# Where the convolution step of a nine-step software pipeline leaves its gap

## The chip, the core and the metric

The kernel runs on one core of a Trainium2 chip. The metric is device time in microseconds (us) of one execution. Engines are named as in the profile: PE (TensorE matmul), PEld (its weight loads), DVE (VectorE), ACT (ScalarE), POOL (GpSimd) and SP (the engine that here only issues DMAs).

## What is computed

The input is x of shape 16 x 16 x 256 x 256 (batch, channel, row, column), float32. Layer 0, a spectral layer, turns it into a new x and is not touched here. Layer 1, reduced to what matters (`gn` normalizes groups of two channels; all convolutions are padded to the same size; `c` runs over 16 channels; `mish(v) = v*tanh(softplus(v))`):

```python
v   = gn(x)                                        # 16 batches, 16 channels
f   = mish(conv3x3(each channel of v alone, W1))   # 4 features a channel
top, bot = f[rows 0..127], f[rows 128..255]
ker = Wspan * relu(1x1(bot, Wred)) + bspan         # 9 weights for each pixel
ti  = sum over the 9 taps of patches(top) * ker    # the "involution"
shuffled = concat_rows(ti, roll(bot, -1, channel)) # 64 planes of 256 x 256
out = mish(conv3x3(shuffled, W2))                  # the second convolution
gate = sigmoid(conv over channels(mean(out), Weca))# one number a channel
x   = x + v * gate
```

So a batch's gate needs all of the batch's second convolution, and rows of the second convolution need the rows of `ti` and `bot` under them.

## The kernel before, in words

Layer 1 is the function `layer1`. Each batch is cut into nine **units**: unit s covers 30 image rows of the upper half, and the 30 rows 128 further down, of 8 channels; j is the block of rows, h the half of the channels, in the order (0,0), (0,1), (1,0) to (3,1), and then (4,0), the **tail unit** with the last 8 rows for all 16 channels. The tail unit holds half the work of another.

A unit passes through these parts, each a method of `Unit`:

- on creation, `load_rows` issues the loads of its input `z` on SP (ten DMAs, 24 for the tail unit);
- `lower`: first convolution of the lower rows (tile `c`, L1037), then Mish on ACT into `bot` (L1056);
- `reduce`: the 1x1 reduction (`pr`, L1064), Relu on ACT into `r`, and `store_bot`, the DMAs on POOL that put `bot` into the DRAM buffer `cf`;
- `upper(0)`, `upper(1)`: first convolution of the upper rows (L1037), with eight Mish activations each into `wide` (L1085);
- `spread`: eight copies on POOL (L1097, L1098) of shifted columns in `wide`;
- `involution(0)` to `(3)`, one for each feature: for each group of four channels a matmul into `pd` (L1105), a DVE multiply into `t` (L1113) and two DVE adds into `top` (L1116); a full unit has eight such groups and the tail unit four. After the last feature `store_top` issues the DMAs into `cf` on POOL (four for a full unit, L1127; 16 for the tail unit, L1134; one more where j is 0).

The **second convolution** of a batch comes in eight pieces of 32 image rows. `conv2_rows(b, s)` loads a piece's rows from `cf` into one of two buffers `rows2` (one DMA of 2176 KB on SP, L1165). `conv2(b, s, acc)` is a generator in three sections: eight matmuls (L1185) and an ACT copy into `mid`, and half of the sum `pair` on DVE (L1175); then 16 matmuls, DVE `even` and `both`, the other half of `pair`; then 16 matmuls on `pair`, and DVE `odd` (L1212). `pooled` puts Mish over `even` and `odd` and adds their sums to `acc` (L1196).

The **gate** of a batch sums `acc` (L1221), spreads the sum (L1223), multiplies by the channel weights (`pg`, L1237), and takes a sigmoid by a chain of small DVE operations (L1239 to L1245). Then POOL scales the stored x in four pairs of parts `o` (L1253) and writes the output (L1262).

The order on every engine but SP is the program's order, written out by hand in one loop; nothing is rescheduled. Step i of the loop has b, s = divmod(i, 9). In it `now` is unit i, which is in its involution, and `nxt` is unit i+1, which is in its first convolution; the loads of unit i+2 are issued at its start. In between stand the sections of one piece of the second convolution: piece s of batch b-1 in steps s = 0 to 7. In step 8 there is no piece, and the gate of batch b-1 begins. The parts of the step stand in the order lower, involution(0), first section, reduce, upper(0), involution(1), second section, upper(1), spread, involution(2), third section, involution(3). The last batch has its pieces in steps of their own, after all units are done.

PSUM tiles: `c` has two buffers, `pd`, `pr` and `pg` share three (tag "d", pool `psd`), and `c2ps` has one. `top`, `bot` and `z` are double buffered by unit (`z` with two tiles a unit).

Of the kernel before, what the change touches and what calls it, by code (L numbers as in the profile page):

```python
# [10 lines left out]
F32 = mybir.dt.float32  # L11
# [10 lines left out]
P = 128  # L22
# [910 lines left out]
def layer1(ctx, tc, d, zn, cf, mr, nb):  # L933
# [14 lines left out]
    sm = ctx.enter_context(tc.tile_pool(name="l1s", bufs=2))  # L948
# [213 lines left out]
    def conv2_rows(b, s):  # L1162
        t = rows2[(8 * b + s) % 2]
        flat = cf[b % 4].rearrange("(t y) f c x -> (y f c) t x", y=2)
        nc.sync.dma_start(out=t[:, :, 1 : N + 1], in_=flat[:, 16 * s : 16 * s + 17])  # L1165

    def conv2(b, s, acc):

        t = rows2[(8 * b + s) % 2]

        def sums(lo, hi):
            nc.vector.tensor_tensor(  # L1175
                pair[:, lo:hi], t[:, lo:hi, H + 1 :], t[:, lo:hi, : H + 1], ALU.add
            )

        def products(terms, n=0):
            pool, tag = (psd, "d") if n % 2 and b == nb - 1 else (ps2, "c2")  # L1180
            ps = pool.tile([P, 4, H], F32, tag=tag, name="c2ps")
            for i, (w, src, x) in enumerate(terms):
                for blk in range(2):
                    for j in range(4):
                        nc.tensor.matmul(  # L1185
                            ps[32 * j : 32 * j + 32],
                            lhsT=w[:, blk],
                            rhs=src[:, 4 * j + blk : 4 * j + blk + 4, x : x + H],
                            start=(i, blk) == (0, 0),
                            stop=(i, blk) == (len(terms) - 1, 1),  # L1190
                        )
            return ps

        def pooled(y, q):
            k = 2 * s + q
            nc.scalar.activation(y, y, AF.Mish, bias=b2, accum_out=acc[:, k : k + 1])  # L1196

        a = mid[s % 2]
        nc.scalar.copy(a[:, :, :H], products([(c2[:, :, 1], t, H + 1)]))
        sums(0, 9)  # L1200
        yield
        ps = products([(c2[:, :, 0], t, 0), (c2[:, :, 2], t, 1)], 1)
        even = rp.tile([P, 4, H], F32, tag="even", name="even", bufs=2)
        nc.vector.tensor_tensor(even, ps, a[:, :, :H], ALU.add)  # L1204
        both = rp.tile([P, 4, H], F32, tag="both", name="both", bufs=2)
        nc.vector.tensor_tensor(both, ps, a[:, :, 1:], ALU.add)  # L1206
        sums(9, 17)
        yield
        pooled(even, 0)
        ps = products([(c2[:, :, 0], pair, 0), (c2s, pair, 1)])  # L1210
        odd = rp.tile([P, 4, H], F32, tag="odd", name="odd", bufs=2)
        nc.vector.tensor_tensor(odd, ps, both, ALU.subtract)  # L1212
        yield
        pooled(odd, 1)
        yield
# [59 lines left out]
    def begin_unit(i):  # L1275
        if i < len(order):
            b, s = order[i]
            units[i] = Unit(b, i, *blocks[s])

    E = mybir.EngineType  # L1280
    with tc.manual_schedule(engines={E.PE, E.Activation, E.DVE, E.Pool}):
        begin_unit(0)
        begin_unit(1)
        u = units[0]
        u.lower()
        u.reduce()
        u.upper(0)
        u.upper(1)
        u.spread()
        acc, last, second = None, iter(()), iter(())  # L1290
        for i in range(9 * nb + 12):
            b, s = divmod(i, 9)
            now, nxt = units.pop(i, None), units.get(i + 1)
            begin_unit(i + 2)
            if s == 8 and b < nb:
                conv2_rows(b, 0)
            if s < 7 and b and b <= nb:
                conv2_rows(b - 1, s + 1)
            next(last, None)
            if nxt:  # L1300
                nxt.lower()
            next(second, None)
            second = iter(())
            if s == 8 and b and b <= nb:
                last = gate(b - 1, acc)
                next(last)
            if s < 8 and b and b <= nb:
                if s == 0:
                    acc = sm.tile([P, 16], F32, tag="acc", name="acc")
                second = conv2(b - 1, s, acc)  # L1310
            if now:
                now.involution(0)
            next(second, None)
            if nxt:
                nxt.reduce()
            if s == 8:
                next(last, None)
            if nxt:
                nxt.upper(0)
            if now:  # L1320
                now.involution(1)
            next(second, None)
            if nxt:
                nxt.upper(1)
                nxt.spread()
            if now:
                now.involution(2)
            if s == 8:
                next(last, None)
            next(last, None)  # L1330
            next(second, None)
            if now:
                now.involution(3)
# [159 lines left out]
@with_exitstack  # L1493
def forward(ctx, tc, d):
    nb = d["x"].shape[0]
    dram = ctx.enter_context(tc.tile_pool(name="dram", bufs=1, space=DRAM))
    keep = ctx.enter_context(tc.tile_pool(name="keep", bufs=1))
    al = dram.tile([NF, 2, 64, nb, N], F32, name="al")
    bd = dram.tile([nb, P, P], F32, name="bd")
    hd = dram.tile([2, 2, 64, nb, C, N], F32, name="hd")  # L1500
    tabs = (
        dram.tile([P, 2, C, N], F32, name="td"),
        dram.tile([NF, P, 384], F32, name="avd"),
        dram.tile([P, 2, C, N], F32, name="ed"),
    )
    zn = dram.tile([nb, N + 2, C, N + 2], F32, name="zn")
    cf = dram.tile([4, N + 2, 4, C, N], F32, name="cf")
    mr = keep.tile([P, nb, G, 2], F32, name="mr")
    layer0_forward(tc, d, al, bd, tabs)
    layer0_mix(tc, d, al, hd, tabs)  # L1510
    layer0_back(tc, d, hd, bd, zn, mr, tabs[2])
    layer1(tc, d, zn, cf, mr, nb)
# [25 lines left out]
```

## Time and profile before

| what | us |
|---|---|
| median of 3 runs | 7067.28 (7063.57 to 7080.53) |
| the profiled execution | 7081.88, its span 7080.1 |
| layer 1 begins, about | 3560 |
| a full step, second convolution in it | 24.29 |
| a batch's nine steps | 211.5 to 214.3 |

The span is the time from the first to the last recorded instruction. A profile line of a group gives its source line, engine, operation, tiles (out<-in), shape and count, then the busy time, the mean duration, and the idle time of the engine before it with what ended it. In a timeline each row is a run of equal instructions: its start, the time from its start to its end, engine, line and tiles, and in brackets the idle time before it. One matmul of the program appears as two instructions of the chip; some records are missing.

### The profile page before, as it was taken

What the parts mean: (1) busy time and instruction counts of PE and PEld (TensorE: products, weight loads), DVE (VectorE), ACT (ScalarE), POOL (GpSimd) and SP (SyncE); (2) the same over time, 40 slices, a digit from 0 to 9 for tenths busy, and PEclk for the clock granted to TensorE, in tenths of its full rate; (3) what the DMA queues carried; (4) which work ended last, traced back from release to release, by engine and by line L of the source; (5) the groups of instructions that cost most, each with busy time, mean ns of one, the idle gap of its engine ahead of it and who ended that gap; (6) DMA issues with size and microseconds to landing.
All of it is one profiled execution on the core that took longest, in us unless ns stands there. A gap on an engine that the chain in (4) does not pass through costs nothing. (4 is left out here: it accounts for less than half of the span.)

```text
span 7080.1 us, 144599 instructions
## 1 busy us (share of the span) xinstructions
PE 6544.7 (92%) x55592; PEld 3663.3 (52%) x55592; DVE 5608.9 (79%) x10346; ACT 3835.5 (54%) x5996; POOL 3521.3 (50%) x4614
## 2 busy tenths in 40 slices
PE   7889999899999998899979999999999999999996
PEld 5777778666667666677733333333333333333331
DVE  8999985466667666688878888888888888888885
ACT  2223333365666665322266666666666676666671
POOL 2334445412222222466655666667666667665663
PEclk9899999999999999999989999999999999999998
DMA  3344444433333333699968888889888889888886
GB/s 99 112 115 123 125 120 123 132 95 92 100 99 102 98 96 92 207 326 326 326 191 248 260 257 269 277 278 282 268 257 265 277 281 278 277 258 264 277 272 212
DMA packets 716083, 1443.41 MB, mean 204 GB/s; under 512 B 98954, under 2 KB 525254, under 8 KB 673638
## 3 DMA queue, kind: packets, MB, share of 16 engines
q1 hardware_dynamic: 567206, 959.76, 44.3%
q0 software_dynamic: 148192, 474.40, 21.3%
q8 instruction: 444, 7.27, 0.4%
q14 instruction: 241, 1.97, 0.1%
HBM read 877.12 MB, written 556.47 MB: 202 GB/s over the span
## 5 line engine op out<-in xcount | busy, mean ns | idle before, releaser
L1085 ACT ACTIVATE wide<-c,b 32x512 f32<-32x512 f32 x2176 | 1477.6, 679 | 314.0 <-PE c L1037 265.2
L1116 DVE TENSOR_TENSOR top<-pd,t 32x512 f32<-32x512 f32 x2176 | 1504.0, 691 | 55.8 <-DMA cf<-top 3.2
L1037 PE MATMUL c<-z,w 102*128 102x512 f32 x2048 | 996.4, 618 | 110.5 <-ACT wide L1085 89.0
L1113 DVE TENSOR_TENSOR t<-pd,r 64x512 f32<-64x512 f32 x1088 | 743.8, 684 | 349.0 <-PE pd L1105 322.8
L1097 POOL COPY wide<-wide 32x1031 f32<-32x1031 f32 (+1 forms) x576 | 581.2, 1009 | 882.6 <-ACT wide L1085 855.5
L1105 PE MATMUL pd<-wide,dw 128*128 128x512 f32 x2048 | 994.4, 607 | 13.0 <-DVE top L1116 12.0
L720 POOL DMA_DIRECT2D hd<-h x512 | 323.5, 639 | 1207.1 <-DVE h L713 1182.6
L1037 PEld LDWEIGHTS c<-z,w 102*128 102x128 f32 x2048 | 370.6, 191 | 695.2 <-issue 457.9
L1185 PE MATMUL c2ps<-rows,c 128*32 128x512 f32 x6144 | 721.9, 602 | 5.6 <-DVE odd L1212 5.6
L1105 PEld LDWEIGHTS pd<-wide,dw 128*128 128x128 f32 x2048 | 382.8, 193 | 576.5 <-issue 417.2
L1056 ACT ACTIVATE bot<-c,b 128x512 f32<-128x512 f32 x544 | 343.9, 683 | 462.2 <-issue 383.3
L1098 POOL COPY wide<-wide 32x1031 f32<-32x1031 f32 (+1 forms) x576 | 574.0, 997 | 33.5
L700 PE MATMUL ph<-ix,yt 64*128 64x256 f32 x4128 | 506.6, 393 | 6.1 <-issue 5.4
L643 PE MATMUL ps<-tt,lt 128*64 128x256 f32 x4224 | 495.4, 385 | 13.3 <-DMA tt<-td 10.4
L313 PE MATMUL px<-wxn,u 128*64 128x256 f32 x4224 | 482.9, 380 | 8.1 <-ACT o L320 8.1
L207 PE MATMUL pu<-fy,eo 128*128 128x128 f32 x2048 | 427.0, 292 | 26.4 <-DVE u L224 21.8
L700 PEld LDWEIGHTS ph<-ix,yt 64*128 64x128 f32 x4128 | 395.9, 191 | 93.7 <-issue 46.1
L1185 PEld LDWEIGHTS c2ps<-rows,c 128*32 128x32 f32 x6144 | 175.4, 109 | 513.3 <-issue 407.8
L873 POOL TENSOR_TENSOR x<-x,o 128x512 f32<-128x512 f32 x256 | 323.7, 1265 | 217.4 <-DVE o L872 199.3
L607 DVE TENSOR_SCALAR alb<-alc,m 128x1024 f32<-128x1024 f32 x330 | 420.0, 1397 | 0.0
L214 PE MATMUL pv<-at,eo 128*128 128x128 f32 x2048 | 413.9, 285 | 0.0
L651 DVE COPY s<-ps 128x512 f32<-128x512 f32 x264 | 265.4, 1023 | 186.9 <-PE ps L643 169.7
(220 smaller groups left out, 11732.0 us busy)
## 6 DMA issues: line engine op xcount, KB each, us to landing
rows<-cf SPq DMA_DIRECT2D x128, 2176.0 KB
z<-zn SPq DMA_DIRECT2D x768, 257.8 KB
cf<-top POOLq DMA_DIRECT2D x512, 240.0 KB, 6.8
cf<-bot POOLq DMA_DIRECT2D x96, 840.0 KB, 11.0
alc<-al SPq DMA_DIRECT2D x264, 256.0 KB
zn<-zb SPq DMA_DIRECT2D x128, 516.0 KB
o<-zn SPq DMA_DIRECT2D x128, 516.0 KB
z<-in_x SPq DMA_DIRECT2D x64, 1024.0 KB
```

The source lines that it names most:

```text
L207: nc.tensor.matmul(pu[:, xh, e].rearrange("p v m -> p (v m)"), lhsT=lhs, rhs=fy[:, e], start=True, stop=True,)
L313: nc.tensor.matmul(ps[64 * k : 64 * k + 64, :, h], lhsT=u[:, h, part, g0 + j + k].rearrange("p f c -> p (f c)"), rhs=wxn[:, h, part], star ...
L643: nc.tensor.matmul(ps[64 * h : 64 * h + 64, v], lhsT=lt[:, h, k, 1 - v : 3 - v].rearrange("p l f c -> p (l f c)"), rhs=tt[:, h, k], start= ...
L700: nc.tensor.matmul(ph[q][:, e], lhsT=yt[lanes, i].rearrange("p t k -> p (t k)"), rhs=ix[lanes, i], start=n == 0, stop=n == 3,)
L1037: nc.tensor.matmul(ps[:, a], lhsT=w, rhs=z[:k, c : c + 2, 0:N], start=True, stop=True)
L1085: nc.scalar.activation(self.feat[64 - 32 * q : 96 - 32 * q, f, self.groups[g], :H], ps[q][32 * f : 32 * f + 32], AF.Mish, bias=b1[0][32 * ...
L1097: nc.gpsimd.tensor_copy(flat[0:32, f, 1:m], flat[64:96, f, 0 : m - 1])
L1098: nc.gpsimd.tensor_copy(flat[96:128, f, 0 : m - 1], flat[32:64, f, 1:m])
L1105: nc.tensor.matmul(ps, lhsT=dwt if self.tail else dw, rhs=self.feat[:, f, cs, :H], start=True, stop=True,)
L1113: nc.vector.tensor_tensor(t[64:128], ps[:64], self.r[:, cs], ALU.mult)
L1116: nc.vector.tensor_tensor(self.top[32 * f : 32 * f + 32, cs, q], ps[lanes], t[lanes], ALU.add)
L1185: nc.tensor.matmul(ps[32 * j : 32 * j + 32], lhsT=w[:, blk], rhs=src[:, 4 * j + blk : 4 * j + blk + 4, x : x + H], start=(i, blk) == (0, 0 ...
```

## The change

The pieces of the second convolution move one step towards the units. Piece 0 of batch b stands in step 8 of batch b itself, beside its tail unit, and pieces 1 to 7 in steps 0 to 6 of the next batch. The step without a piece is step 7 in place of step 8, and the gate's sections move with it. The loads of the rows move by one step, too: pieces 0 and 1 are loaded in steps 7 and 8, and pieces 2 to 7 in steps 0 to 5. The loop is one step shorter. No compute instruction or DMA is added or removed; their order changes, and on SP and POOL the DMAs of `rows`, `o` and the output move past those of the units.

```diff
-        for i in range(9 * nb + 12):
+        for i in range(9 * nb + 11):
             b, s = divmod(i, 9)
             now, nxt = units.pop(i, None), units.get(i + 1)
             begin_unit(i + 2)
-            if s == 8 and b < nb:
-                conv2_rows(b, 0)
-            if s < 7 and b and b <= nb:
-                conv2_rows(b - 1, s + 1)
+
+            if s >= 7 and b < nb:
+                conv2_rows(b, s - 7)
+            if s < 6 and b and b <= nb:
+                conv2_rows(b - 1, s + 2)
             next(last, None)
             if nxt:
                 nxt.lower()
             next(second, None)
             second = iter(())
-            if s == 8 and b and b <= nb:
+            if s == 7 and b and b <= nb:
                 last = gate(b - 1, acc)
                 next(last)
-            if s < 8 and b and b <= nb:
-                if s == 0:
-                    acc = sm.tile([P, 16], F32, tag="acc", name="acc")
-                second = conv2(b - 1, s, acc)
+            if s == 8 and b < nb:
+                acc = sm.tile([P, 16], F32, tag="acc", name="acc")
+                second = conv2(b, 0, acc)
+            if s < 7 and b and b <= nb:
+                second = conv2(b - 1, s + 1, acc)
             if now:
                 now.involution(0)
             next(second, None)
             if nxt:
                 nxt.reduce()
-            if s == 8:
+            if s == 7:
                 next(last, None)
             if nxt:
                 nxt.upper(0)
...
             if now:
                 now.involution(2)
-            if s == 8:
+            if s == 7:
                 next(last, None)
```

## The prediction

> **What bounds the kernel now.** I read the page first: which engine carries the chain that ended last, and which engines are full.
>
> ```profile
> PE 6544.7 (92%) x55592; PEld 3663.3 (52%) x55592; DVE 5608.9 (79%) x10346; ACT 3835.5 (54%) x5996; POOL 3521.3 (50%) x4614
> PE c2ps L1185 16%; PE c L1037 13%; PE pd L1105 13%; ACT wide L1085 3%; PE pr L1064 2%; DVE top L1116 0%; DVE pair L1175 0%; DVE t L1113 0%; DMA cf<-top 0%; ACT odd L1196 0%; ACT bot L1056 0%; DVE even L1204 0%; POOL o L1253 0%; DVE both L1206 0%; DMA out_dram<-o 0%
> ```
>
> Layer 1 is a chain of its own matmuls; the one other entry of weight is ACT's `wide` (3%). Next come stretches, one for each of steps 6, 7, 8 and 0 at a batch boundary (columns: stretch, length, busy PE, PEld, DVE, ACT, POOL with counts, granted clock, DMA share, GB/s):
>
> ```profile
> 4974.64:4998.93 24.29, 24.29 (x121) 8.35 (x120) 21.02 (x30) 16.86 (x27) 11.29 (x15) 1.00 0.71 229
> 4998.93:5020.52 21.59, 21.59 (x110) 7.41 (x109) 20.75 (x30) 9.49 (x16) 15.78 (x26) 1.00 0.88 261
> 5020.52:5034.83 14.31, 12.59 (x35) 4.86 (x33) 11.66 (x31) 10.05 (x17) 1.56 (x3) 1.00 0.88 292
> 5034.83:5065.74 30.91, 27.26 (x121) 9.44 (x122) 22.36 (x33) 21.56 (x33) 27.28 (x40) 0.89 0.88 245
> ```
>
> Step 6 is pure PE. The loss sits in step 8, which has no piece of the second convolution, and in the step 0 that inherits it. PE's timeline there:
>
> ```profile
> 5020.52 3.60 PE L1037 MATMUL c<-z,w 102*128 102x512 f32 x8
> 5026.78 0.37 PE L1237 MATMUL pg<-wca,totals 128*128 128x16 f32 x2 [0.27 <-DVE totals L1223]
> 5034.83 1.98 PE L1037 MATMUL c<-z,w 102*128 102x512 f32 x4 [1.46 <-ACT wide L1085]
> 5040.47 3.78 PE L1037 MATMUL c<-z,w 102*128 102x512 f32 x4 [3.65 <-ACT wide L1085]
> 5044.04 2.71 PE L1105 MATMUL pd<-wide,dw 128*128 128x512 f32 x4
> ```
>
> ACT has the 16 `wide` of a full unit (5029.18 to 5040.42 in its own timeline) and PE has too little beside them, so it waits 1.46 and 3.65 us for a `c` buffer. The two rows after the long wait cost 3.78 and 2.71 us where the same rows elsewhere cost about 1.8. Fine stretches say why:
>
> ```profile
> 5040.50:5044.00 3.50, 3.50 (x4) 1.47 (x5) 0.00 (x0) 1.20 (x2) 3.33 (x4) 0.50 1.11 356
> 5044.00:5048.00 4.00, 4.00 (x17) 1.29 (x19) 1.95 (x3) 1.26 (x2) 3.55 (x7) 0.79 1.10 334
> ```
>
> After the wait the clock is half for 3 to 4 us.
>
> [...]
>
> **The work without its waits.** A full step is 24.29. Its parts from PE's timeline: a group of `c` 1.72, a `pd` 0.905, the piece 1.77 + 3.61 + 3.57 = 8.95, `pr` 1.0. Step 7 lacks two groups of `c`: 20.85. Step 8 lacks four `pd` (3.62) and the piece and has `pg` (0.33): 12.05. So the nine steps hold 7 x 24.29 + 20.85 + 12.05 = 202.9. The gate's matmul repeats at 211.5 to 214.3 us, median 211.9: 9.0 are lost in each batch (8.6 in the best).
>
> **After, step 7.** Nothing is removed in sum; PE's work of the nine steps stays 202.9. Step 7 now has 20.85 - 8.95 + 0.33 = 12.2 of PE work, and eight groups and the gate on DVE. Durations from DVE's timeline:
>
> ```profile
> 5000.42 0.68 DVE L1113 TENSOR_TENSOR t<-pd,r 64x512 f32<-64x512 f32 x1
> 5002.57 0.68 DVE L1113 TENSOR_TENSOR t<-pd,r 64x512 f32<-64x512 f32 x1
> 5026.15 0.17 DVE L1221 TENSOR_REDUCE total<-acc 128x1 f32<-128x16 f32 x1 [1.75 <-ACT odd L1196]
> 5026.67 0.68 DVE L1113 TENSOR_TENSOR t<-pd,r 64x512 f32<-64x512 f32 x1
> 5028.81 0.17 DVE L1239 TENSOR_SCALAR gate<-pg 128x16 f32<-128x16 f32 x1
> 5032.15 0.68 DVE L1113 TENSOR_TENSOR t<-pd,r 64x512 f32<-64x512 f32 x1
> ```
>
> A group takes 2.15 (5000.42 to 5002.57), `total` and `totals` 0.52, the chain of the sigmoid 3.34 (5028.81 to 5032.15). Counted from the start of step 7: ACT ends the last `odd` at 3.93 (as at 5002.86 now) and DVE ends step 6's groups at 3.64, so `total` starts at about 3.96, and the first group at 4.48; two groups to 8.78; sigmoid to 12.12; groups 3 to 5 to 18.57. The eighth `pd` needs the buffer of the fifth group: it runs from 18.6 to 19.5. So step 7 takes 19.5, of which 7.3 are lost, in pieces: near 2.0 before `pg` (its buffer is the first group's), 2.8 behind the sigmoid, and twice 1.2. The same pattern without the gate stands in batch 0, whose step 7 has no piece even now:
>
> ```profile
> 3731.54 1.88 PE L1037 MATMUL c<-z,w1t 120*128 120x512 f32 x4
> 3747.77 1.10 PE L1105 MATMUL pd<-wide,dw 128*128 128x512 f32 x2 [1.05 <-DVE top L1116]
> 3748.70 3.60 PE L1037 MATMUL c<-z,w 102*128 102x512 f32 x8
> ```
>
> 17.16 us for eight groups of 2.15: DVE sets it, and the clock is 1.00 there.
>
> **After, steps 8 and 0.** Step 8 gets the piece: 24.29 - 3.62 = 20.67. ACT needs 16 x 0.70 + 4 x 0.6 + 2 x 0.7 + 0.6 + 0.9 = 16.5 in it, under PE's 20.7, so the waits for `wide` go; 8.95 us of piece cover the 5.1. DVE enters step 8 6.9 us late (its last group of step 7 ends at 26.4), but has only four groups and 5 us of piece there; the second half of `pair` ends within 0.1 us of need. If this cover failed it would cost the old 1.46 + 3.65. Step 0 is 24.29. Sum of the three steps: 19.5 + 20.7 + 24.3 = 64.5. Now they take 211.9 less six full steps (145.7) = 66.2, or 65.8 in the best batch. So a batch gains 1.3 to 1.7, if the clock stays whole. It may not: [...] A half window that falls within step 7 is hidden behind DVE; one that reaches 1 to 2 us into step 8 costs half of that, up to 0.9. Bounds for the clock: 0 and 0.9 a batch, with nothing to exclude a second half window (1.7 more). I take 0.5, and a gain of 0.9 a batch: 15 boundaries, **-13.5 us**.
>
> **Moved DMAs.** Loads of rows are the trace's only 1024-byte packets of their queue; they end 7 to 27 us before their first matmul in all batches before the last. Pieces 0 to 2 need stores of units 0 to 7, long issued or 14 us ahead. Piece 3 is the exposed one: its load needs the tail unit's `top`, and is issued at step 1 where it was step 2. POOL in step 8: eight copies of `spread` (8.8) from 16.8 us after the step's start, where `upper(1)` begins to give `wide`, to 25.6; two scaled parts and output DMAs (6.6, from 5044.44 to 5051.09 now), then the 16 stores (9.5, from 5051.09 to 5060.6), to 42 and landing 4 later: 46, where step 1 starts at 45. SP stands some 8 us at that load, with `o` and the next `z` behind it, which are needed 20 us later. A load takes 9 to 20 us from there, in the trace's packets, and PE wants it at 74: slack 8 to 19. Costed at nothing; beyond that slack each us late costs 1 us in each batch. `top`'s buffer is reused at 49.8, 4 us behind these stores.
>
> **The end.** Now from step 8 of the last batch (6929.31) to the second piece (6956.56): 27.25 us. After: the second piece starts when the first one's `odd` is done. DVE reaches 34.6 (from step 7's start) with the halves of `pair`, PE needs 3.6, `odd` 1: 39.3, which is 19.8 after step 7. That saves 7.4; a half clock takes 1, and piece 3's load, which starts right behind the tail's stores even now (first packet 6969.2, last store issued 6965.8; 2.5 us slack), about 3. Bounds 0 and 8; I take **-3.5 us**.
>
> Sum -17. The profiled execution (7081.88) is 14.6 over the median, and some 7 of that lie in four batches with longer periods; the gain is the same on both, so from the median: 7067.3 - 17 = **7050**; from the profiled one 7065.
>
> **Rivals.**
> 1. *The trade is even*: the clock loss returns in step 8 (0.9 and some of a second window) and eats the batch gain; only 0 to 5 us at the end remain: 7064. For it: a 2.8 us gap; against: batch 0 held 1.00 with gaps of 1.05.
> 2. *Better*: the clock never drops and the irregular longer periods (up to 214.3) go with the step-8 knot: 15 x 1.7 + 7 = 32: 7035. Against: one of those is a wait for a store (`top` behind DMA, 3.2 us) in the middle of a batch.
> 3. *Slower, by POOL's late tail stores*: at step 1, piece 3's load, if the stores land 8 to 19 us later than worked out, PE waits. To lose 0.3% this has to cost (21 + 17)/15 = 2.5 us a batch beyond the slack; at 4 us it is 7067 + 60 - 17 = 7110. For it: DMA is full (share 1.02) in the gate's steps, POOL is overfull in step 8 (25.9 us of work in 20.7). Against: POOL is more overfull now (14.3) and catches up in one step.
>
> **Chances.** Forecast 0.48 (own range 7036 to 7062), rival 1 0.24, rival 2 0.12, rival 3 0.16. A change under 0.3% (21 us; bounds 7046 and 7088) can't be told from none. Faster: rival 2 and near half of the forecast: 0.34. Slower: most of rival 3: 0.14. The range 7030 to 7088 leaves out the rest of rival 2 and of rival 3.
>
> **What would show it.** Right: PE's waits for `wide` in step 8 gone; in step 7 waits for `top` and for the gate of 1 to 3 us, step 7 near 19.5 and step 8 near 20.7; period near 210.5 to 211. Half clock inside step 7 or absent. Wrong: a step 7 over 21, PE waiting for `rows` or for `spread` in steps 1 or 2, or a half clock well inside step 8.

## The result and the profile after

| | before | after |
|---|---|---|
| median | 7073.90 us (4 runs, 7063.57 to 7082.51) | 7124.31 us (4 runs, 7113.31 to 7128.94) |
| the profiled execution, its span | 7081.88, 7080.1 | 7128.94, 7127.1 |
| a batch's nine steps, mean of batches 2 to 14 | 212.1 | 215.6 |

The ratio is 1.0068, with a 95% interval of 1.0056 to 1.0080. The change made the kernel slower by 50 us, where 17 us of gain were forecast.

**Engines and chain.** First the page of the kernel after: the line of busy times, and the chain that ended last.

```profile
PE 6556.4 (92%) x55592; PEld 3657.8 (51%) x55592; DVE 5604.6 (79%) x10346; ACT 3835.4 (54%) x5996; POOL 3502.2 (49%) x4614
...
PE c2ps L1185 13%; PE c L1037 11%; PE pd L1105 10%; DVE top L1116 2%; DMA cf<-top 2%; PE pr L1064 1%; DMA out_dram<-o 1%; POOL o L1253 1%; DVE t L1113 1%; POOL wide L1098 1%; POOL wide L1097 1%; ACT wide L1085 0%; POOL cf L1134 0%; DVE exp_n L782 0%; ACT bot L1056 0%
```

The work is the same. What is new is in the chain: ACT's `wide` (3% before) is gone, and in its place stand the stores of `top`, the output DMA, POOL's scaling of `o` and POOL's copies in `wide`. All of these are POOL's, or issued by POOL. DVE's `top` has risen from 0 to 2%.

**Where the time goes.** Stretches of the kernel after, one for each of steps 7, 8, 0 and 1 at one batch boundary (stretch, length, busy PE, PEld, DVE, ACT, POOL with counts, granted clock, DMA share, GB/s):

```profile
5233.17:5252.79 19.62, 14.50 (x31) 4.99 (x30) 18.09 (x41) 8.07 (x13) 13.32 (x23) 0.91 1.02 330
5252.79:5273.64 20.85, 20.85 (x113) 6.84 (x112) 16.49 (x25) 14.98 (x23) 13.36 (x21) 1.00 1.02 327
5273.64:5297.92 24.28, 24.28 (x122) 8.45 (x120) 19.95 (x27) 18.06 (x30) 18.00 (x28) 1.00 0.92 292
5297.92:5330.40 32.48, 27.32 (x122) 8.95 (x121) 21.05 (x30) 16.86 (x27) 24.95 (x34) 0.89 0.88 252
```

The first three rows are what the forecast worked on, and at this boundary they are as forecast: 19.62, 20.85 and 24.28. It is an extreme case: its steps 7 and 8 are among the shortest, and its step 1 loses the most of all batches. The loss is in the last row, step 1, which has no part in the edit's gap: 32.48 us for a step of 24.28, of which 5.16 are idle and 3.0 are matmuls at half clock (27.32 busy where 24.28 is the work). Averaged over batches 2 to 14 (from one unit's first `bot` to the next one's, on ACT), the steps read:

```
step        8      0      1      2      3      4      5      6      7      sum
before    17.95  26.62  24.28  24.47  24.28  24.27  24.28  24.28  21.72   212.14
after     20.84  24.27  26.82  25.98  24.28  24.28  24.27  24.28  20.63   215.64
```

Steps 7, 8 and 0 together gained 0.55 by this count. Steps 1 and 2 lost 4.2 us over a clean 24.28 each. They lose in batches 2 to 15, so 14 x 4.2 = 59 us. In batch 1, which has no gate running into it from the batch before, they lose nothing. Added up over the 14 batches, step 1 loses 39 us and step 2 22 (the kernel before loses 2.7, once). In five of them the wait brings half clock with it; these five lose 6.0 to 8.2 us each, 33 us of the 61.

**What PE waits for in step 1.** PE's timeline of the kernel after, two rows from the start of that step:

```profile
5297.92 3.60 PE L1037 MATMUL c<-z,w 102*128 102x512 f32 x8
...
5306.68 3.78 PE L1105 MATMUL pd<-wide,dw 128*128 128x512 f32 x4 [5.16 <-POOL wide L1098]
```

The first `pd` of the step waits 5.16 us for POOL's copies in `wide` (`spread`), and then its matmuls take 3.78 us where 1.8 is usual. So POOL is late. Its timeline before, from the output DMAs in step 8 to the next unit's `spread` (step 8 began at 5020.52):

```profile
5050.28 0.81 POOL L1262 DMA_DIRECT2D out_dram<-o  x1 [0.30 <-POOL o L1253]
5051.09 3.04 POOL L1134 DMA_DIRECT2D cf<-top  x6
5054.82 0.51 POOL L1134 DMA_DIRECT2D cf<-top  x1 [0.69 <-DMA out_dram<-o]
5056.11 4.47 POOL L1134 DMA_DIRECT2D cf<-top  x9 [0.78 <-DMA out_dram<-o]
5060.57 1.06 POOL L1157 DMA_DIRECT2D cf<-bot  x2
5061.68 1.03 POOL L1097 COPY wide<-wide 32x1031 f32<-32x1031 f32 x1
```

And the same stretch of POOL's timeline after (step 8 began at 5252.79):

```profile
5284.92 0.81 POOL L1262 DMA_DIRECT2D out_dram<-o  x1 [0.30 <-POOL o L1253]
5285.73 3.05 POOL L1134 DMA_DIRECT2D cf<-top  x6
5290.58 0.51 POOL L1134 DMA_DIRECT2D cf<-top  x1 [1.81 <-DMA out_dram<-o]
5294.60 4.03 POOL L1134 DMA_DIRECT2D cf<-top  x8 [3.51 <-DMA out_dram<-o]
5300.05 0.50 POOL L1134 DMA_DIRECT2D cf<-top  x1 [1.43 <-DMA cf<-top]
5300.55 0.54 POOL L1157 DMA_DIRECT2D cf<-bot  x1
5303.92 0.54 POOL L1157 DMA_DIRECT2D cf<-bot  x1 [2.83 <-issue]
5304.50 1.03 POOL L1097 COPY wide<-wide 32x1031 f32<-32x1031 f32 x1
```

The same instructions stand in the same order in both: two outputs, the tail unit's 16 stores, two stores of `bot`, then the copies that PE needs. The difference is in the brackets. Issues on POOL waited for an earlier DMA to land (0.69 and 0.78 us before; 1.81, 3.51 and 1.43 after), and everything behind them on POOL waited too, copies included. The earlier DMA is nearly always the one eight issues before: in layer 1 of these two traces POOL never has more than eight DMAs issued and not yet landed, and 134 of the 138 such waits in the kernel after end within 0.5 us of that landing (74 of 75 before). These eight are the "slots" of the expectations below; whether the chip or the program sets them is not shown. So the ninth DMA from the first output on, here the tail unit's seventh store, stood for 1.81 us, until that output had landed. Counted from the start of step 8:

| POOL | before | after | adds to the delay |
|---|---|---|---|
| the 16 stores begin | 30.6 | 32.9 | +2.3 |
| the 16 stores are issued | 40.1 | 47.8 | +5.4 |
| `spread` begins | 41.2 | 51.7 | +2.8 |

Step 1 starts at 45 in both, and its first `pd` wants the copies at about 48.8. Before, they were there with about 5 us to spare (first two copies done at 43.3); after, they are 5 us late. In the mean of batches 1 to 14 the 16 stores take 9.1 us before and 14.1 after, and `spread` begins at 41.9 and 48.8. The 2.8 us of the last row, a wait for which the profile shows no releaser, belong to this boundary. Output DMAs land in 8.1 us before and 9.5 after, with DMA shares of 0.88 in step 8 before and 1.02 in steps 7 and 8 after.

**What PE waits for in step 2.** Here it is another waiter on the same queue. Late copies and scaled parts also put off the stores of unit 0's `top`, which stand behind them on POOL, and DVE needs that buffer again in step 2 of the loop. Batch 10 of the kernel after, whose step 2 starts at 5757.20 and loses 2.5 us:

```profile
5750.56 2.04 POOL L1127 DMA_DIRECT2D cf<-top  x4
5766.57 1.39 DVE L1116 TENSOR_TENSOR top<-pd,t 32x512 f32<-32x512 f32 x2 [3.71 <-DMA cf<-top]
5768.11 1.10 PE L1105 MATMUL pd<-wide,dw 128*128 128x512 f32 x2 [0.51 <-DVE top L1116]
5770.25 1.10 PE L1105 MATMUL pd<-wide,dw 128*128 128x512 f32 x2 [1.05 <-DVE top L1116]
```

DVE waits 2.2 to 4.5 us in this way in the ten batches whose step 2 loses time, and at most 1.0 in the four that lose nothing there. Before, it happened once (3.2 us).

### The profile page after: what moved, and what is told of

Read it like the earlier page. It is cut to its first block, busy times and chain, and to the rows that moved or that the text cites. A ratio compares the mean times of both kernels' runs of the same rounds, so it can differ in the third digit from the quotient of the medians.

```text
span 7127.1 us, 144607 instructions
## 1 busy us (share of the span) xinstructions
PE 6556.4 (92%) x55592; PEld 3657.8 (51%) x55592; DVE 5604.6 (79%) x10346; ACT 3835.4 (54%) x5996; POOL 3502.2 (49%) x4614
## 4 chain that ended last, share of the span: by engine, by line
PE 35%; DVE 4%; POOL 4%; DMA 4%; issue 2%; ACT 1%; SPq 0%; POOLq 0%; DVEq 0%; ACTq 0%
PE c2ps L1185 13%; PE c L1037 11%; PE pd L1105 10%; DVE top L1116 2%; DMA cf<-top 2%; PE pr L1064 1%; DMA out_dram<-o 1%; POOL o L1253 1%; DVE t L1113 1%; POOL wide L1098 1%; POOL wide L1097 1%; ACT wide L1085 0%; POOL cf L1134 0%; DVE exp_n L782 0%; ACT bot L1056 0%
## 5 line engine op out<-in xcount | busy, mean ns | idle before, releaser
L1116 DVE TENSOR_TENSOR top<-pd,t 32x512 f32<-32x512 f32 x2176 | 1504.2, 691 | 89.9 <-DMA cf<-top 37.7
L1105 PE MATMUL pd<-wide,dw 128*128 128x512 f32 x2048 | 1028.2, 621 | 119.7 <-DVE top L1116 87.6
L1037 PE MATMUL c<-z,w 102*128 102x512 f32 x2048 | 982.6, 612 | 33.3 <-DMA z<-zn 20.8
L207 PE MATMUL pu<-fy,eo 128*128 128x128 f32 x2048 | 430.8, 294 | 26.8 <-DVE u L224 21.5
```

The lines of the kernel that those rows point to most:

```text
L207: nc.tensor.matmul(pu[:, xh, e].rearrange("p v m -> p (v m)"), lhsT=lhs, rhs=fy[:, e], start=True, stop=True,)
L1037: nc.tensor.matmul(ps[:, a], lhsT=w, rhs=z[:k, c : c + 2, 0:N], start=True, stop=True)
L1105: nc.tensor.matmul(ps, lhsT=dwt if self.tail else dw, rhs=self.feat[:, f, cs, :H], start=True, stop=True,)
L1116: nc.vector.tensor_tensor(self.top[32 * f : 32 * f + 32, cs, q], ps[lanes], t[lanes], ALU.add)
```

## The experiments

Three theories stood at the start.

- **A**: the gate's output DMAs stand ahead of the tail's stores on POOL, and the stores wait for them to land; put elsewhere or taken out, the stall goes.
- **B**: the stall comes with the pieces' new place (their row loads now fill DMA around the tail unit); it stays wherever the gate and its outputs stand.
- **C**: it is POOL's own time, the scaling of `o` above all, that makes `spread` late.

The expectations call runs 1, 2, 5 and 6 below e1, e2, f1 and f0. All diffs are against the kernel after, unless said otherwise; where one lengthens the loop, the steps added at its end do nothing but finish the generator of the last gate.

**1. The pieces moved, the gate left in step 8.**

```diff
-        for i in range(9 * nb + 11):
+        for i in range(9 * nb + 12):
...
-            if s == 7 and b and b <= nb:
+            if s == 8 and b and b <= nb:
                 last = gate(b - 1, acc)
...
-            if s == 7:
+            if s == 8:
                 next(last, None)
```

(the last two lines in both places)

> The pieces of the second convolution stand as in the changed kernel, the gate and its parts stay in step 8 as before. Theory A (what the changed kernel lost is POOL's: the tail unit's 16 stores wait for in-flight slots behind the gate's output DMAs, which the change put a step earlier into a full DMA, and the next spread stands behind them): with the outputs back in their old steps the 4.4 us a batch that PE lost in steps 1 and 2 mostly go, and step 7 loses the sigmoid's 3.3 us and the wait for the sum as well (from 19.6 to about 15.3 to 16): 64.75 - 3.6 = 61 for steps 7, 8 and 0, a batch of about 207, and a time of 6985 to 7010, faster than before. Theory B (the row loads, moved beside the tail unit, fill the DMA and hold the stores whatever the gate does): step 7 is short too, but steps 1 and 2 keep 3 to 5 us of waits a batch: 7045 to 7065.

Measured: 7062.88 us, 0.9986 of the kernel before (0.9977 to 0.9994). By the number this is B's. But the sum hides two things: step 7 falls to 16.1 us, and steps 1 to 3 still lose 4.4 us over clean ones. So the stall is there with the outputs back where they were, which A had not foreseen. The order of parts and stores on POOL is that of the kernel before, where `spread` had some 5 us of slack; with the piece in step 8 and its row loads a step earlier this slack is used up: the 16 stores take 13.7 us (batches 1 to 14), nearly the 14.1 of the kernel after. So most of their lengthening comes with the pieces' move, and not with the earlier outputs. PE's waits for POOL's copies, from the list of waits between 3950 and 6900 us (what waits, for what: us in total, times, longest), of this kernel:

```profile
PE pd L1105 <- DVE top L1116: 56.0, 61, 2.3
PE pd L1105 <- POOL wide L1098: 21.1, 19, 4.0
```

and of the kernel after:

```profile
PE pd L1105 <- DVE top L1116: 70.0, 39, 3.6
PE pd L1105 <- POOL wide L1098: 28.2, 19, 5.2
```

19 waits for the copies in both; the kernel before has none of note. DVE's waits for stores to land, to reuse `top`, are 63.7 us here and 37.7 in the kernel after.

**2. The gate in step 7, its scaled parts one step later.** In `gate`, behind `scale`:

```diff
         nc.vector.tensor_tensor(scale, gate, std2[:, b], ALU.add)
         yield
+        yield
+        yield
         for k in range(0, 8, 2):
...
-        for i in range(9 * nb + 11):
+        for i in range(9 * nb + 12):
```

> The changed kernel, with two empty turns after the gate's sigmoid, so that the scaling and the output DMAs come one step later, in the steps they had before; sum, sigmoid and pieces stay in step 7 and 8. Theory A: the stalls of steps 1 and 2 shrink from 4.4 to under 1.5 us a batch: 7124 less 45 to 65, so 7060 to 7080. Theory B: no change, 7115 to 7130. Step 7 stays at 19.6 us in both.

Measured: 7100.19 us, 1.0039 (1.0025 to 1.0053), between the two. Steps 1 to 3 lose 2.4 us instead of 4.2. PE's waits for copies fall from 28.2 to 9.8 us, but DVE's waits to reuse `top` do not (48.5 us). One step is not enough: the first two outputs still stand ahead of the tail's stores, which take 11.8 us, and the next two ahead of the copies issued in step 1.

**3. No output.** This leaves out the output DMAs of batches 0 to 14; the scaling stays.

```diff
-                nc.gpsimd.dma_start(out=dst.rearrange("c y x -> y c x"), in_=o[:, :, 1 : N + 1])
+                if b == nb - 1:
+                    nc.gpsimd.dma_start(
+                        out=dst.rearrange("c y x -> y c x"), in_=o[:, :, 1 : N + 1]
+                    )
```

> The changed kernel without the output DMAs of the first 15 batches (their result is not written; all else, the scaling on POOL too, stays). Theory A: with the outputs out of the in-flight slots the 16 stores take about 9 us, spread is in time, PE's stalls in steps 1 and 2 go: 7124 - 60 = 7060 to 7070. Theory C (POOL has simply too much work of its own in step 8, slots or not): 3 us of the 10 us of delay go with the issues, the stalls stay near 3 us a batch: 7095 to 7115.

Measured: 7067.19 us, 0.9989 (0.9980 to 0.9998). Steps 1 and 2 are clean (24.30 and 24.28). A's number, though not quite A's reason: the 16 stores begin 3.2 us earlier, but take 12.6 us, where 9 were expected. C's number is missed, and all the scaling is still on POOL.

**4. No scaling.** This leaves out POOL's scaling in batches 0 to 14; the outputs stay, unscaled.

```diff
-                for i in range(4):
-                    eng = nc.vector if i and b == nb - 1 else nc.gpsimd
+                for i in range(4 if b == nb - 1 else 0):
+                    eng = nc.vector if i else nc.gpsimd
```

> The changed kernel without POOL's scaling of x in the first 15 batches (the parts are written out as they were loaded; all DMAs stay). POOL has 4.4 us less before the tail unit's stores. Theory C: the delay of spread falls by those 4.4 us and the stalls nearly go: 7065 to 7080. Theory A: the output DMAs are issued earlier but land late all the same, and half of the 4.4 us comes back as waits for slots: 7080 to 7105.

Measured: 7068.97 us, 0.9991 (0.9983 to 1.0000), and steps 1 and 2 lose only 0.25 us. That is C's number, not A's. Read with the run before it: either of the two, taken away, is enough. Here the waits of POOL's issues for outputs to land rose (the tail's stores 69.0 us in all, where after has 52.8; the 16 take 17.2 us), and yet `spread` was on time, because the scaling ahead of it was gone and the stores began 6.3 us earlier. So neither theory alone is right. What counts is the sum in POOL's queue ahead of `spread`: scaling, issues and waits for landings together.

**5. The gate in step 7, its parts from step 0 on.** Four yields in place of the two of run 2, and a loop of `9 * nb + 13`. No part or output stands ahead of the tail's stores any more; the row loads stay where the kernel after has them.

> The changed kernel with four empty turns after the sigmoid: scaling and output DMAs come in steps 0 to 3 of the next batch, two steps later than in the changed kernel, so that in step 8 POOL has only the spread and the tail unit's stores. Theory A/C (POOL's queue in step 8): the tail's stores begin 6.6 us earlier and find the slots free, the next spread is in time, PE's waits in steps 1 and 2 (4.2 us a batch) go to under 0.7: 7124 - 55 = 7060 to 7075, as without outputs. Theory B (the DMA engines are full in these steps whatever POOL does, and e2 only spread it): waits of 2 us or more stay, and come in steps 2 to 4: 7090 to 7105. Step 7 stays near 20.6.

Measured: 7063.52 us, 0.9985 (0.9978 to 0.9991) of a kernel before of 7075.10. Steps 1 and 2 are 24.27 each. POOL's timeline of this kernel, tail's stores to `spread`:

```profile
5250.87 3.99 POOL L1134 DMA_DIRECT2D cf<-top  x8
5259.01 2.00 POOL L1134 DMA_DIRECT2D cf<-top  x4 [4.15 <-DMA cf<-top]
5261.28 2.00 POOL L1134 DMA_DIRECT2D cf<-top  x4 [0.27 <-issue]
5263.28 1.07 POOL L1157 DMA_DIRECT2D cf<-bot  x2
5264.62 1.03 POOL L1097 COPY wide<-wide 32x1031 f32<-32x1031 f32 x1 [0.27 <-ACT wide L1085]
```

The stores still wait 4.2 us for a landing, now that of the first of them, eight issues earlier, but they start behind `spread`'s last copy, with no part in between, and the next copies wait for ACT and not for POOL. B as it stands falls: the row loads are all here, and the stores take 12.4 us (9.1 before), but begin 7.7 us earlier than in the kernel after, so PE loses nothing in steps 1 and 2, and DVE no longer waits to reuse `top`. Against this kernel, the one after is slower by 60.8 us by the medians (and 63.4 by the spans), which is the 59 us of steps 1 and 2.

**6. The same with the gate in step 8**, that is runs 1 and 5 together: step 8 for the gate, two extra yields, and a loop of `9 * nb + 13`.

> The kernel of e1 (pieces moved, gate in step 8) with two empty turns after the sigmoid: scaling and output in steps 0 to 3. Theory A/C: e1's short step 7 (16.1) stays, and its 4.4 us of waits in steps 1 to 3 go to about 1: a batch near 208.5, 7063 - 45 = 7010 to 7025, faster than both kernels. Theory B: a batch that is shorter by PE's sum meets a full DMA, waits of 3 to 4 us stay: 7050 to 7065.

Measured: **7002.31 us** (4 runs, 6999.22 to 7013.02), **0.9895** (0.9875 to 0.9916). It beats both kernels. Against run 5 step 7 falls from 20.8 to 16.3 and step 8 rises from 20.8 to 21.5: 3.8 us a batch, which is close to the DVE time of the gate worked out in the prediction (3.34 for the sigmoid's chain and 0.52 for the sums), moved from a step that DVE bounds into one with over 4 us of DVE to spare (step 8 of the kernel after: 16.49 us busy in 20.85). PE's timeline of this kernel in step 7 and at the gate in step 8:

```profile
5194.15 1.10 PE L1105 MATMUL pd<-wide,dw 128*128 128x512 f32 x2 [0.88 <-DVE top L1116]
...
5198.44 2.04 PE L1105 MATMUL pd<-wide,dw 128*128 128x512 f32 x2 [1.05 <-DVE top L1116]
5200.28 4.33 PE L1037 MATMUL c<-z,w 102*128 102x512 f32 x8
5208.14 0.40 PE L1237 MATMUL pg<-wca,totals 128*128 128x16 f32 x2
```

The waits are in pieces of 1 us, and `pg` waits for nothing.

**7. The control: the kernel before, with the parts later.** Two extra yields and a loop of `9 * nb + 13` in the kernel before.

> The kernel before with the two empty turns of f0: sum, sigmoid and pieces as before, scaling and output one step later, in steps 0 to 3. If f0's gain comes from the moved pieces with POOL kept clear, this alone does little, since before has no wait for spread at the boundary: 7060 to 7078. If the later outputs are a gain by themselves: 7000 to 7040.

Measured: 7069.35 us, 0.9997 (0.9991 to 1.0004). Later parts alone gain nothing; they only matter once step 8 holds a piece.

**8. Is the wait behind the sigmoid dear beyond its length?** Run 5, with three matmuls that nobody reads in step 7, behind `involution(1)`. They go to the buffer of `c2ps`, which is free in that step.

```diff
             if now:
                 now.involution(1)
+            if s == 7 and 0 < b < nb:
+                spare = ps2.tile([P, 4, H], F32, tag="c2", name="spare")
+                for _ in range(3):
+                    nc.tensor.matmul(
+                        spare, lhsT=dw, rhs=now.feat[:, 0, 0:4, :H], start=True, stop=True
+                    )
```

> The kernel of f1 (changed, parts from step 0) with three idle matmuls of 128 x 512 in step 7 after involution(1), into the free buffer of c2ps; nothing reads them. They fill 2.6 of the 3.6 us for which PE waits behind the sigmoid. If the half clock that follows this wait is what makes step 7 last 20.8 where the durations on DVE add up to 19.6: the half clock goes, step 7 falls to about 19.7, and the time from 7063.5 to about 7047 in spite of more work on PE. If the step is longer for another reason: 7063 to 7070.

Measured: 7045.24 us (4 runs, 7042.32 to 7056.64), 0.9962 (0.9947 to 0.9977), 18 us under run 5 by the medians, 16 by the ratios to the kernel before; the two profiled executions differ by 9, this one's being the slowest of its four. PE's timeline of run 5 behind the sigmoid:

```profile
5220.53 1.81 PE L1105 MATMUL pd<-wide,dw 128*128 128x512 f32 x2 [3.59 <-DVE top L1116]
5222.67 1.85 PE L1105 MATMUL pd<-wide,dw 128*128 128x512 f32 x2 [0.33 <-DVE top L1116]
```

and of this one:

```profile
5216.45 2.74 PE L1331 MATMUL spare<-wide,dw 128*128 128x512 f32 x6
5219.02 1.02 PE L1105 MATMUL pd<-wide,dw 128*128 128x512 f32 x2
5221.06 1.10 PE L1105 MATMUL pd<-wide,dw 128*128 128x512 f32 x2 [1.01 <-DVE top L1116]
```

The spare matmuls fill the gap, the same `pd` takes 1.02 in place of 1.81, and the half-clock time between 3800 and 6900 us (from the trace's clock records) falls from 81.9 to 20.5 us. Step 7, from its first `c` to the next, is 19.6 in 9 of the batches 1 to 14 and 20.4 or 20.5 in the other 5; in run 5 it is 19.6 in only 4.

## Why the prediction was wrong

**Step 7: right but for the clock, wrong in its pieces.** Forecast 19.5, measured 19.6 where the clock is whole at its end. But PE's waits are not 2.0, 2.8 and twice 1.2. PE's timeline of the kernel after, from `pr` to the next step:

```profile
5236.92 1.05 PE L1064 MATMUL pr<-bot,wr 128*32 128x512 f32 x4 [0.15 <-DVE top L1116]
5238.76 0.40 PE L1237 MATMUL pg<-wca,totals 128*128 128x16 f32 x2 [0.78 <-ACT r L1073]
...
5247.57 3.89 PE L1105 MATMUL pd<-wide,dw 128*128 128x512 f32 x4 [3.62 <-DVE top L1116]
5251.86 1.10 PE L1105 MATMUL pd<-wide,dw 128*128 128x512 f32 x2 [0.41 <-DVE top L1116]
5252.79 3.60 PE L1037 MATMUL c<-z,w 102*128 102x512 f32 x8
```

The wait ahead of `pg` is 0.78, and the one behind the sigmoid 3.62, with half clock behind it: four matmul instructions in 3.89 us, where 1.88 is usual. A fine stretch of the same trace:

```profile
5247.50:5251.00 3.50, 3.30 (x4) 0.97 (x4) 3.39 (x5) 0.00 (x0) 3.21 (x6) 0.52 0.85 233
```

DVE hides this inside step 7 unless the half clock reaches the step's end; then step 7 takes 20.5 (8 of the 14 batches 1 to 14), and step 8, too, begins at half clock. The mean of step 7 is 20.2.

**Steps 8 and 0: right with a whole clock.** 20.85 and 24.28, for 20.7 and 24.3. The waits for ACT's `wide` (71.5 us in all before) are gone. But the mean of step 8 is 21.3 (20.8 to 22.0 from its first `c` to the next step's), since the half clock runs into it. So the clock costs 0.6 in step 7 and 0.4 in step 8: 1.0 a batch, where 0.5, its author's estimate, was taken. This term was mis-sized, and a batch gains 0.5 in these steps, for 0.9. A hint stood in the prediction's own stretches: the half clock that it read as 3 to 4 us lasts from 5038.88 to 5045.70, 6.8 us, in the trace's clock records, 5.2 of them after the wait.

**The end: right.** From step 7 of the last batch to the second piece of the last convolution it was 48.8 us and is 43.1: 5.7 saved, where 3.5 for the end and 2.1 for step 7 itself make 5.6. From there on both kernels take 123.5 us.

**"Moved DMAs ... Costed at nothing": this step failed.** It saw POOL's queue in step 8, with the copies ending at 25.6 (measured 25.1) and the parts at 32.2 (measured 32.9). Then it went wrong twice. It priced the 16 stores at 9.5 us, as they had stood before, and so had them issued at 42; with their waits for landings they were issued at 47.8 (on average they took 14.1 us). And it asked who waits for these stores (the row load of piece 3, the reuse of their own `top`), but not who stands behind them on POOL: the next unit's `spread`, whose slack was only 5 us, and behind that the stores of unit 0's `top`, which DVE awaits in step 2. In place of nothing this cost 59 us. PE waiting for `spread` in steps 1 or 2 does stand among the prediction's signs of being wrong, and it came true, but the working gave that wait no time and no slack. The waits for landings stood on POOL itself, 3.51 us of them for one output, ahead of the copies behind it.

The row load of piece 3 was no cause: in all batches before the last the rows are 3.5 to 25 us ahead of their first matmul. `top` was the smaller of the two causes, with step 2's 22 us against step 1's 39; DVE's waits to reuse it came to 37.7 us, where before had 3.2.

**Rival 3** had the place (the tail's stores on POOL) and the wrong waiter. That its size fits (4 us a batch, 7110) is luck: it was an example, not worked out. What was held against it, that POOL is overfull before too and catches up in one step, was the weak argument: before, it caught up because the tail's stores waited only 1.5 us.

**The account.** The profiled executions differ by 47.0 us. By PE's first `c` of each step, +59.1 of it lie in steps 1 and 2 of batches 2 to 15, -7.0 in steps 7, 8 and 0 at the 14 boundaries behind batches 1 to 14 (-0.5 each), +2.1 at the boundary behind batch 0, where no gate runs and the piece is only added, -5.8 from step 7 of the last batch on, and -1.4 ahead of all this.

**What stays open.** Run 1 shows that the 16 stores take nearly as long (13.7 us for 14.1) with the outputs in their old steps. What it is in the pieces' move that lengthens them, the row loads beside the tail unit or the changed lengths of the steps, was not separated. Run 5 shows only that without the parts ahead it costs nothing.

## What to carry to other kernels

When DMAs are issued from an engine that also computes, price its whole queue: here an issue's wait for a landing was a wait of every copy and store behind it, and at the boundary shown the waits of the tail's stores came to 1.5 us before and 6.8 after, with a DMA share of 0.51 while they were issued before (5051.09 to 5060.57) and 0.77 after (5285.73 to 5300.55). When a piece of work moves, look for who stands behind on each queue and what slack that waiter has, besides who reads the data; here the queue had two such waiters. And move only what gains from it: the second convolution gained from the tail unit's step, while the gate lost in a step that DVE bounds and its outputs lost ahead of the tail's stores; with each in its own place the kernel was 1.05% faster than before.

## What the runs showed of the hardware

**A gap of 3.6 us in PE's work cost more than its length, and useless matmuls in it made the kernel faster**: 7063.5 to 7045.2 us (0.9985 and 0.9962 of the kernel before). In the traces of the kernels before and after, the half clocks start on a grid of 3.41 us; a stretch of 3.41 us from one point of it to the next is called a window here. Between 3800 and 6900 us there are 33 such starts (14 before, 19 after), and in the window ahead of each PE had been idle for 1.70 to 3.41 us, so mostly not for the whole window; of the windows at full clock that no half clock followed, none had more than 1.78 us of idle time. So about half a window of idle time, in one piece or several, was enough in these two kernels (matmul ends are modelled in the trace, which blurs the limit). In the kernel before, the half clock at 5038.88 us, which the prediction puts down to a wait of 3.65 us, began when 2.06 us of that wait had passed. Each of the 33 half clocks lasted one window or two (3.41 or 6.83 us). In run 6, whose waits in step 7 shown above are of 0.88 and 1.05 us, half clock came to 27 us between 3800 and 6850 us, where its last unit begins; up to 6900 us the kernel before has 58, run 5 82 and the kernel after 113.

**The price of an issue was not a constant.** A DMA issue on POOL took 0.5 us (0.8 for an output), and the tail unit's 16 took 7.9 to 11.9 us before and 12.5 to 16.7 after, with the waits for landings inside (batches 0 to 14). At most eight were under way, as seen above, and an output landed 9.5 us after its issue (median of the kernel after): the two ahead of the tail's stores held up the eighth issue behind each, by 1.81 and 3.51 us at the boundary shown.
